# A fused graph and attention network on one core: the heads stage makes two steps of its side work per round in tiles 0 to 7

## The chip, the cores and the metric

The kernel runs on one NeuronCore of a Trainium2 chip. The core has a matrix engine (TensorE, in profiles PE, with its weight loads shown as PEld), VectorE (DVE), ScalarE (ACT), GpSimd (POOL) and SyncE (SP), which here only issues transfers. Each engine runs its own instructions in program order, and waits on semaphores for the others. The metric is the device time of one execution in microseconds; lower is better. A comparison is made on medians of several executions.

## The reference

The input is a node matrix `x` of 3327 x 256 and a symmetric 0/1 adjacency `adj` of 3327 x 3327. Four sublayers follow, each with a residual and a layernorm before it: a normalised graph convolution, a mixture of 8 experts with the top 2 chosen, a graph attention, and the last one, which concerns us, a causal attention with 4 heads of width 64, each with 4 query experts:

```python
sx = jnp.einsum('bsh,ndh->bnsd', x, hl_w) + hl_b[None, :, None, :]
q = jnp.einsum('bnsd,neod->bneso', sx, wq)      # 4 experts of queries per head
k = jnp.einsum('bnsd,nod->bnso', sx, wk)
v = jnp.einsum('bnsd,nod->bnso', sx, wv)
scores = jnp.einsum('bnesd,bntd->bnest', q, k) * d ** 0.5 + causal
qkv = jnp.einsum('bnest,bntd->bnesd', jax.nn.softmax(scores, axis=-1), v)
qkv = jnp.where(pad[:, :, None], 0.0, qkv)      # pad = (sx == 0)
gs = softmax(out @ gate_w + gate_b)             # gate over the 4 experts
mixed = jnp.einsum('bnsed,bnse->bnsd', out.reshape(b, nh, s, ne, d), gs)
hn = layernorm(mixed + resid, ln_g, ln_b)
# two dense layers on each head's 64 numbers with masks at exact zeros,
# a layernorm, and a softmax gate over the 4 heads
```

## The kernel before

The nodes are padded to 26 tiles of 128 rows (`NT` = 26, `P` = 128). The stages run one after another; the last, `heads` (line 773), takes the time from about 985 us to the end. All its instructions are recorded through `InOrder`, so every engine executes them in exactly the order in which the Python code issues them. For this reason almost all of them show the same line, L61, in the profile, and are told apart by tile names.

The work of the stage is a list of units, one for each tile `t` of 128 query rows and each of the 4 heads. A unit is cut into chunks of 512 keys (`BLK`), `t // 4 + 1` of them, because attention is causal: tiles 0 to 3 have one chunk per head and four per tile, tiles 4 to 7 have two per head and eight per tile, and so on, 392 in all. One turn of the main loop at line 1263, called a round here, handles chunk `k`, with several chunks in flight:

- `fill` (line 972): TensorE makes the scores of the 4 experts into four PSUM tiles `pqk`, from the tile's queries `qt` and the keys `kt`; the causal mask is added by small products (`own`, `after`).
- `drain` (994): VectorE copies each from PSUM to `sc` and takes the maximum on the way (the TENSOR_SCALAR_CACHE_REDUCE rows); at the unit's last chunk the maxima are joined to `anmax`.
- `weigh` (1014): ScalarE takes exp in place, with sums into `aden`.
- `values` (1028): SP issues the loads `vr<-vs` of the chunk's values from DRAM.
- `turn` (1035): VectorE transposes the weights in 32 x 32 blocks (STREAM_TRANSPOSE).
- `attend` (1047): TensorE multiplies them with the values into `po`.
- `over` (1066) at a unit's last chunk: ScalarE copies `po` to `ot`, and POOL multiplies by the mask `sxd`.
- `back` (1076), one round after it: TensorE turns `ot` back with the gate's weights (`ptO`), and ScalarE copies it to `qkv` and `glp`. At head 3 a tail is begun; before that, tails are run on until at most two are left.

The order in a round `k` is: the drains up to `wanted(k)` (three chunks ahead, more where a unit has more chunks), `attend` of chunk `k`, `turn` of chunk `k + 1`, `values` and half of `weigh` of chunk `k + 2`, `back` of a unit ended the round before, `over` of a unit ended now, a step of the side work, the rest of `weigh`, and a `fill` if none is waiting to be drained. `fill` of a tile's first chunk first calls `begin` (1217).

The side work is written as Python generators, and `run` (line 964) takes each of a list one step further, up to its next `yield`:

- `prepare(t)` (line 880), in the list `preps`, makes the projections of the next tile in 9 steps: 1 the load `xres` from DRAM; 2 layernorm statistics on VectorE and a root on POOL (`prs`); 3 the normalised rows `xn` on VectorE; 4 their transpose on TensorE (`pt`, copied to `xt`); 5 `psxt` and, on ScalarE, `sxt`; 6 four transfers to `sxd` and the product `pv` (copied to `v`); 7 `pk` (copied to `kt`) and four transfers of `v` to `vs` in DRAM; 8 `pq` (scaled into `qt`); 9 the compare that makes `sxd` a mask, and a transpose of `sxt` to `sx`. `begin` of a tile first runs `preps` to the end, and then begins the projections of the tile after it.
- `tail(t)` (line 1138), in `tails`, finishes a tile in 17 steps: the gate's softmax (`ard`, `glp`, `gl`, `gsm`, `gss`), the weighted sum over experts on POOL (`qkv`, `fx`), a layernorm (`l1st` on VectorE, the rest on POOL), two dense layers (`ph`, `h`, `fo`) with the masks, a second layernorm (`l2st`), the gate over heads (`fot`, `pfg`, `fgm`, `fgs`) with the residual's load `xend`, and the store of the result. Some steps are empty, to leave POOL time.

In tiles 0 to 7 the side work makes one step in every round; from tile 8 on, only in rounds that do not follow a unit's end. PSUM tiles of all these products (`pqk`, `pt`, `psxt`, `pv`, `pk`, `pq`, `ptO`, `ph`, `pfg`) share four buffers in rotation (pool `psm`), so each product waits until the fourth tile before it has been emptied. The helper `empty` (856) gives a copy out of PSUM to ScalarE or VectorE, by a running sum of costs that the code keeps.

Of the kernel before, what the change touches and what calls it, by code (L numbers as in the profile page):

```python
# [101 lines left out]
class Net:  # L102
# [670 lines left out]
    def heads(self, xs, vs, out):  # L773
# [3 lines left out]
        with ExitStack() as ctx:  # L777
# [186 lines left out]
            def run(gens):  # L964

                gens[:] = [g for g in gens if next(g, None) is None and g.gi_frame is not None]

            tails, preps, ready = [], [], {}
# [45 lines left out]
            def weigh(u, g, experts):  # L1014

                n = min(BLK, (u["t"] + 1) * P - g * BLK)
                q = ready[u["t"]]
                if u["h"] == g == 0 and 0 in experts:
                    q["den"] = sm.tile([P, 16, 7], F32, tag="den", name="aden", bufs=3)
                for k in experts:  # L1020
                    e = u["sc"][g][:, k, :n]
                    nc.scalar.activation(
                        e, e, AF.Exp, bias=u["nmax"][:, k : k + 1],
                        accum_out=q["den"][:, 4 * u["h"] + k, g : g + 1],
                    )
                    load["act"] += 0.26 + 0.00088 * n

            def values(u, g):

                n = 4 * min(4, u["t"] + 1 - 4 * g)  # L1030
                v = u["v", g] = vrp.tile([P, 16, 64], F32, tag="vr", name="vr")
                for q in range(4):
                    nc.sync.dma_start(out=v[ds(Q * q, Q), :n, :], in_=vs[u["h"], g, :, :n, :])

            def turn(u, g):


                n = min(BLK, (u["t"] + 1) * P - g * BLK)
                w = u["sc"][g][:, :, :n]
                nc.vector.transpose(w, w)  # L1040
                load["dve"] += 0.1 + 0.00417 * n
# [5 lines left out]
            def attend(u, g):  # L1047


                t = u["t"]  # L1050
                w, v = u["sc"][g], u["v", g]
                n = 4 * min(4, t + 1 - 4 * g)
                for b2 in range(0, n, 2):
                    for k in range(2):
                        for q in range(4):
                            r, b = ds(Q * q, Q), b2 + k

                            after = 4 * t + q - 16 * g
                            if b > after and t:
                                continue  # L1060
                            nc.tensor.matmul(
                                po[ds(64 * k, 64), q, :, :], v[r, b, :], w[r, :, ts(b, Q)],
                                start=(g == b2 == 0), stop=(b + 2 > after if t else b2 == 2),
                            )

            def over(u):

                u["ot"] = tl.tile([P, 4, P], F32, tag="ot", name="ot", bufs=1)
                nc.scalar.copy(u["ot"].rearrange("p e (q i) -> p q e i", q=4), po)
                nc.gpsimd.tensor_tensor(  # L1070
                    u["ot"], u["ot"],
                    u["sxd"][:, u["h"] : u["h"] + 1, :].to_broadcast([P, 4, P]), ALU.mult,
                )
                load["act"] += 0.6

            def back(u):


                h = u["h"]
                r = ready[u["t"]]  # L1080
                if h == 0:
                    r["qkv"] = tl.tile([P, 4, 4, 64], F32, tag="qkv", name="qkv", bufs=2)
                    r["glp"] = sm.tile([P, 4, 4, 4], F32, tag="glp", name="glp")
                pt = ps.tile([P, 4, 68], F32, tag="b", name="ptO")
                for e in range(4):
                    nc.tensor.matmul(
                        pt[:, e, :], u["ot"][:, e, :], igw[:, h, e, :], start=True, stop=True
                    )
                nc.scalar.copy(r["qkv"][:, h, :, :], pt[:, :, :64])
                nc.scalar.copy(r["glp"][:, h, :, :], pt[:, :, 64:])  # L1090
                load["act"] += 0.55
                if h == 3:
                    while len(tails) > 2:
                        run(tails)
                    tails.append(tail(u["t"], u["sx"], r["qkv"], r["glp"], r["den"]))
# [136 lines left out]
            def fill_next():  # L1232
                nonlocal filled
                if filled < len(chunks):
                    u, g = chunks[filled]
                    if g == 0:
                        begin(u)
                    fill(u, g)
                    filled += 1

            def drain_to(n):
                nonlocal drained
                while drained < min(n, len(chunks)):
                    if filled == drained:
                        fill_next()
                    drain(*chunks[drained])
                    drained += 1

            def wanted(k):

                return k + 3 + chunks[min(k + 2, len(chunks) - 1)][0]["t"] // 4
# [11 lines left out]
            for k, (u, g) in enumerate(chunks):  # L1263
                ahead = chunks[k + 2] if k + 2 < len(chunks) else None
                drain_to(wanted(k))
                attend(u, g)
                if k + 1 < len(chunks):
                    turn(*chunks[k + 1])
                if ahead:
                    values(*ahead)  # L1270
                    if ahead[1]:
                        weigh(*ahead, range(2))
                if ended:
                    back(ended)
                last = u if g == u["t"] // 4 else None
                if last:
                    over(u)
                if not ended or u["t"] < 8:
                    run(tails)
                    run(preps)  # L1280
                ended = last
                if ahead:
                    weigh(*ahead, range(2 if ahead[1] else 0, 4))
                if filled == drained:
                    fill_next()
# [556 lines left out]
```

## Time and profile before

| what | us |
|---|---|
| runs, not profiled | 3131.43, 3135.38, 3141.88 (median 3135.38) |
| the profiled execution's own time | 3144.19 |
| its span, first to last instruction | 3142.5 |
| PE busy | 2762.7 (88%) |
| DVE busy | 2494.8 (79%) |
| ACT busy | 1671.4 (53%) |
| POOL busy | 891.0 (28%) |

The span is what the profile's rows share out; 1.7 us of the execution's own time lie outside it. Busy time of an engine is the time with an instruction of its own in work. Matmuls are pipelined and their ends are modelled, so a high busy share of PE does not mean that PE sets the pace. PEclk is the share of full speed that TensorE's clock was granted.

### The profile page before, as it was taken

Reading aid. Unit: us, or ns where it says so; the run is one execution under the profiler, and the core shown is the slowest. Engines: PE = TensorE matmul, PEld = TensorE weight load, DVE = VectorE, ACT = ScalarE, POOL = GpSimd, SP = SyncE. Lnnn points to the kernel's source line nnn. Section 1 sums busy time; section 2 is a strip of 40 time slices with the busy share of each in tenths; the row PEclk is TensorE's granted clock in tenths of the full one; section 3 lists DMA queues with packets and bytes.
Section 4 is the critical chain, followed back from the end, with each engine's and each line's share of the span. In section 5 each row is a group of like instructions: output and inputs, shape, how many; then the busy total and the mean of one; then the engine's idle time right before and its main releaser. Section 6 shows DMA issues by size and latency. Waiting matters only on the chain.

```text
span 3142.5 us, 126717 instructions
## 1 busy us (share of the span) xinstructions
PE 2762.7 (88%) x54254; PEld 2025.9 (64%) x54254; DVE 2494.8 (79%) x6166; ACT 1671.4 (53%) x4566; POOL 891.0 (28%) x1208
## 2 busy tenths in 40 slices
PE   7999978688986879989999998889898899999884
PEld 6878877576775656666666666556665566656553
DVE  6104533799995768999998998899998899999994
ACT  6410145555553545666665665556655656566653
POOL 6432544611122353433322221121211111211112
PEclk9999999899998879999999999999999999999997
DMA  9994477476853313333333333333333333333331
GB/s 374 356 292 145 161 261 245 163 264 229 284 187 84 82 50 101 96 95 109 109 96 106 106 107 99 93 107 109 109 101 105 102 102 107 112 105 106 107 106 54
DMA packets 258193, 449.80 MB, mean 143 GB/s; under 512 B 58816, under 2 KB 159680, under 8 KB 257504
## 3 DMA queue, kind: packets, MB, share of 16 engines
q1 hardware_dynamic: 241232, 416.77, 43.5%
q0 software_dynamic: 6576, 18.02, 1.5%
q8 instruction: 428, 7.01, 1.0%
q10 hardware_dynamic: 9824, 6.91, 0.8%
q14 instruction: 133, 1.09, 0.1%
HBM read 393.37 MB, written 25.88 MB: 133 GB/s over the span
## 4 chain that ended last, share of the span: by engine, by line
DVE 37%; PE 23%; ACT 3%; issue 2%; POOL 1%; DMA 0%; SPq 0%; POOLq 0%; DVEq 0%; ACTq 0%
DVE sc L61 33%; PE po L61 10%; PE pqk L61 8%; PE ptO L61 2%; ACT sc L61 2%; PE pq L61 1%; DVE l2mv L61 0%; PE pt L61 0%; DVE gl L61 0%; PE psxt L61 0%; PE ph L61 0%; DVE l1mv L61 0%; DVE fo L61 0%; DVE l2st L61 0%; POOL fo L61 0%
## 5 line engine op out<-in xcount | busy, mean ns | idle before, releaser
L61 ACT ACTIVATE sc<-sc,anmax 128x512 f32<-128x512 f32 (+3 forms) x1568 | 1041.3, 671 | 125.1 <-DVE anmax L61 125.0
L61 DVE TENSOR_SCALAR_CACHE_REDUCE sc<-pqk 128x512 f32<-128x512 f32 (+3 forms) x1568 | 898.6, 627 | 110.6 <-PE pqk L61 109.2
L61 PEld LDWEIGHTS po<-sc,vr 32*64 32x64 f32 x43728 | 683.1, 134 | 369.8 <-DVE sc L61 203.5
L61 PE MATMUL po<-sc,vr 32*64 32x128 f32 x43728 | 789.0, 281 | 122.0 <-DVE sc L61 60.4
L61 PE MATMUL pqk<-kt,qt 64*128 64x512 f32 (+3 forms) x3136 | 832.5, 585 | 57.0 <-DVE fo L61 19.3
L61 DVE STREAM_TRANSPOSE sc<-sc 128x2048 f32<-128x2048 f32 (+3 forms) x392 | 816.0, 2082 | 11.5 <-ACT sc L61 11.3
L61 PEld LDWEIGHTS pqk<-kt,qt 64*128 64x128 f32 x3136 | 320.8, 188 | 295.8 <-issue 118.9
L61 PE MATMUL acc<-wh,p 128*128 128x259 f32 x1352 | 309.3, 386 | 34.4 <-DVE p L61 34.3
L61 POOL TENSOR_TENSOR ot<-ot,sxd 128x512 f32<-128x512 f32 x104 | 132.9, 1278 | 690.4 <-ACT ot L61 660.2
L61 PE MATMUL acc<-y,pan 128*128 128x256 f32 x1352 | 302.5, 384 | 12.3 <-DMA pan<-in_adjt_dram 10.6
L61 PEld LDWEIGHTS acc<-wh,p 128*128 128x128 f32 x1352 | 253.3, 190 | 92.6 <-DVE p L61 52.5
L61 ACT ACTIVATION_READ_ACCUMULATOR sc<-sc,anmax 128x1 f32 x1568 | 303.1, 193 | 0.0
L61 PEld LDWEIGHTS acc<-y,pan 128*128 128x128 f32 x1352 | 256.9, 192 | 53.4 <-issue 18.4
L61 ACT ACTIVATE u<-u,d 128x512 f32<-128x512 f32 (+1 forms) x182 | 125.2, 688 | 158.5 <-DVE u L61 158.3
L61 ACT COPY qkv<-ptO 128x256 f32<-128x256 f32 x104 | 38.7, 373 | 281.5 <-PE ptO L61 281.5
L61 DVE SCALAR_TENSOR_TENSOR u<-bc,d 128x512 f32<-128x512 f32 (+1 forms) x182 | 135.9, 747 | 0.1
L61 DVE SCALAR_TENSOR_TENSOR p<-pan,u 128x512 f32<-128x512 f32 (+1 forms) x182 | 125.8, 691 | 10.5 <-PE acc L61 6.1
L61 DVE DVE_READ_ACCUMULATOR sc<-pqk 128x1 f32 x1568 | 129.6, 83 | 0.0
L61 PE MATMUL ptO<-igw,ot 128*128 128x68 f32 x832 | 118.4, 286 | 11.5 <-DVE sc L61 4.4
L61 PEld LDWEIGHTS ptO<-igw,ot 128*128 128x128 f32 x832 | 103.8, 196 | 31.4 <-issue 21.8
L61 ACT ACTIVATE junk<-ar 128x1664 bf16<-128x1664 f32 x52 | 82.7, 1591 | 66.1 <-DMA ar<-in_adj_dram 64.8
L61 POOL TENSOR_TENSOR qkv<-qkv,gss 128x1024 f32<-128x1024 f32 x26 | 50.1, 1926 | 211.7 <-DVE gss L61 200.9
(286 smaller groups left out, 2870.2 us busy)
## 6 DMA issues: line engine op xcount, KB each, us to landing
vr<-vs SPq DMA_DIRECT2D x1248, 128.0 KB
ar<-in_adj_dram SPq DMA_DIRECT2D x104, 832.0 KB
pan<-in_adjt_dram SPq DMA_DIRECT2D x156, 256.0 KB
pan<-in_adjt_dram SPq DMA_DIRECT2D x26, 1024.0 KB
pan<-in_adjt_dram SPq DMA_DIRECT2D x20, 832.0 KB
w1e<-w SPq DMA_DIRECT2D x59, 256.0 KB
vr<-vs SPq DMA_DIRECT2D x96, 96.0 KB
took<-places SPq DMA_DIRECT2D x59, 129.0 KB
```

The source lines that it names most:

```text
L61: made = make(*args, **kw)
```

## The change

Behind `attend` and ahead of `turn`, in rounds of tiles 0 to 7, tails and projections make a step more. The step that was there, later in the round, stays.

```diff
                 drain_to(wanted(k))
                 attend(u, g)
+                if u["t"] < 8:
+                    run(tails)
+                    run(preps)
                 if k + 1 < len(chunks):
                     turn(*chunks[k + 1])
                 if ahead:
```

`run`, `tails` and `preps` are those described above. Nothing else of the kernel is edited. As `empty` decides by sums of costs so far, a few copies out of PSUM go to the other engine with the new order.

## The prediction

> **What bounds the kernel now.** I read the page first (VectorE, "DVE", is busy 79% of the span and carries 37% of the chain that ended last), then the busy time of each engine stretch by stretch, then VectorE's instructions in order of time. In the table by stretch I cut the heads stage at the first transpose (STREAM_TRANSPOSE) of each of the tiles 0 to 7; columns are length, then busy time per engine, granted clock, DMA share, GB/s.
>
> ```profile
> 1010.54:1033.42 22.88, 16.69 (x232) 13.13 (x229) 10.36 (x42) 10.52 (x42) 4.33 (x4) 0.78 0.29 67
> 1033.42:1058.66 25.24, 21.67 (x346) 17.13 (x346) 17.43 (x58) 14.62 (x52) 6.67 (x6) 0.86 0.29 75
> 1058.66:1089.48 30.82, 26.63 (x480) 19.64 (x480) 22.73 (x65) 17.25 (x55) 15.30 (x16) 0.89 0.30 82
> 1089.48:1125.05 35.57, 30.86 (x600) 23.13 (x602) 26.35 (x76) 19.04 (x57) 14.10 (x15) 0.86 0.24 64
> 1125.05:1193.59 68.54, 52.96 (x829) 38.75 (x820) 41.70 (x159) 27.95 (x99) 36.24 (x45) 0.75 0.22 59
> 1193.59:1235.21 41.62, 38.29 (x904) 27.51 (x898) 38.05 (x119) 27.19 (x90) 20.06 (x22) 1.00 0.36 101
> 1235.21:1282.74 47.53, 42.77 (x1031) 29.67 (x1030) 42.80 (x119) 28.95 (x91) 19.77 (x22) 1.00 0.37 100
> 1282.74:1332.97 50.23, 46.96 (x1154) 32.48 (x1154) 47.60 (x127) 30.85 (x91) 19.99 (x22) 1.00 0.36 103
> ```
>
> Tiles 5 to 7 are bound by VectorE (41.62 − 38.05 = 3.6, then 4.7 and 2.6 us idle). Tiles 0 to 4 are not: VectorE idles 12.5, 7.8, 8.1, 9.2 and 26.8 us, 64.4 in all, and TensorE's clock is 0.75 to 0.89 instead of 1.00. The whole change acts on these 322.4 us, a tenth of the kernel. Where the idle time lies is seen in VectorE's instructions in order of time (start, duration, what; in brackets idle time before it and who ended it):
>
> ```profile
> 1048.73 0.42 DVE L61 COPY kt<-pk 128x256 f32<-128x256 f32 x1 [4.90 <-PE pk L61]
> 1050.44 0.69 DVE L61 TENSOR_SCALAR qt<-pq 128x512 f32<-128x512 f32 x1 [1.28 <-PE pq L61]
> 1052.30 0.56 DVE L61 TENSOR_SCALAR_CACHE_REDUCE sc<-pqk 128x384 f32<-128x384 f32 x1 [0.84 <-PE pqk L61]
> ...
> 1079.39 0.43 DVE L61 TENSOR_SCALAR sxd<-sxd 128x512 f32<-128x512 f32 x1 [6.39 <-DMA sxd<-sxt]
> ...
> 1113.66 0.43 DVE L61 TENSOR_SCALAR sxd<-sxd 128x512 f32<-128x512 f32 x1 [6.59 <-DMA sxd<-sxt]
> ...
> 1146.01 0.42 DVE L61 TENSOR_TENSOR fo<-ph,fb 128x256 f32<-128x256 f32 x1 [4.51 <-PE ph L61]
> ...
> 1164.23 0.69 DVE L61 TENSOR_SCALAR_CACHE_REDUCE sc<-pqk 128x512 f32<-128x512 f32 x1 [5.75 <-PE pqk L61]
> ```
>
> The reader is to see one hole per tile at the place where `begin` finishes the next tile's projections in one go (the chain xt, psxt, sxt, pv, pk, pq, qt, one engine waiting for the next), and from 1133 to 1164 us a second kind: `back` runs three tails to make room for a fourth.
>
> **The change, part by part.** It adds and removes no work; it moves steps, and two products change engine. In each of the rounds of tiles 0 to 7 (4·4 + 4·8 = 48) tails and projections get a second step, issued behind `attend` and ahead of `turn`.
>
> *Projections, tiles 1 to 3 and into 4.* A projection has 9 steps. Four rounds lie between two calls of `begin` in tiles 0 to 3, so now 4 steps are spread and 5 are run at once; with two a round 8 are spread, and one (the compare on sxd, the transpose of sxt) is left. What goes at most is VectorE's idle time there: tile 1: 4.90 + 1.28 + 0.84 = 7.0; tile 2: 6.39 + 0.94 = 7.3; tile 3: 6.59 + 0.63 + 0.22 = 7.4; tile 4, where 8 rounds lay between: 4.19 + 1.54 + 0.39 = 6.1 us. Only two rounds precede the first `begin`: there 7 steps were left (waits 0.54 + 1.72 + 5.00 + 0.72 + 0.99 + 0.43 = 9.4), now 5, so 0.54 + 1.72 = 2.3 go. Sum 30.1.
>
> *Tails.* A tail has 17 steps. With one a round in rounds of 4 to a tile, three are unfinished when the fourth comes, and they are run out together. With two a round each is done in 9 rounds and `back` finds at most two. What goes at most: 1.47 + 2.52 + 0.22 + 4.51 = 8.7 of waits inside, and 5.75 + 0.58 = 6.3 at the end, where VectorE waits for pqk behind it. Sum 15.0. Both together 45.1 of the 75.4 us that VectorE idles in tiles 0 to 7.
>
> *What is late next.* (a) The last round of each projection on TensorE: attend 1.19, pk 1.23, ptO 1.1, pq 1.92, ACT's two qt of 0.60, and the first pqk 0.92 before VectorE has something to drain, 7.6 us; beside it VectorE has 4 drains of 0.47 and 0.16 for the maximum, the transpose 1.25 to 1.78, 0.65 of softmax and 0.42 for sxd, 4.6. 3.0 us stay idle for each of the four boundaries: 12. At the warm clock of tiles 5 to 7 they would be under 2 each; where TensorE stays as cold as in the holes (0.56 at 1043.8 to 1048.7) the round before it adds 1 to 2 (psxt 1.79, sxt 0.63, pv 1.22). Bounds 6 to 20. (b) xn now stands ahead of the transpose and half a round behind its statistics, and POOL makes its root behind the tail's normalisation (roots 1.02 and 0.56, products 0.62, 0.62, 0.73, 0.73: 4.3 us) while VectorE has 0.75 of statistics and 1.9 to 2.8 of drains. It waits about 1 us in tiles 2, 3 and 4, and transpose and `attend` behind it wait too. I take 3; bounds 0 and 14 (twice the one xn wait of the trace, 1.72, in each of tiles 2 to 5). (c) In tiles 5 to 7 there is nothing to fill but 10.9 us of idle time in 24 rounds, 0.45 a round; I take no gain and no loss. Bounds: 5 back (the waits for pqk there sum to 4.6) and 6 lost (half as much again as now).
>
> *SP and POOL.* SP issues a projection's 9 transfers (xres 0.42, four sxd of 0.605, four vs of about 0.5) and a tail's xend and out; half of them now precede the round's vr loads, which are for the chunk two rounds on, 7 us or more away: nothing. Without that cover it would be 2.4 us a tile. The xres that landed 2.1 us after its issue (1013.78, used 1015.92) is now read in its own round; SP reaches it ahead of the third chunk's vr loads, 2 us sooner, so nothing again. POOL's tail products now also stand ahead of `ot`; ptO, one round later, covers that. *Emptying PSUM:* VectorE loses one qt (0.69) and one kt (0.42) to ScalarE and gains one sx (about 0.4): −0.7, noise.
>
> *A rule against it.* In tiles 0 to 7 the seven `glp<-glp,ard` took 2.9 us in all where 225 ns is the median, and one of them 1.25, beside `ot` on POOL; with gss and the two roots' sums the excess is about 3.6 us, already in the rows. The Trainium skill, SBUF — State Buffer, "two separate sides", says that a VectorE operation with two SBUF inputs and a GpSimd operation lock a shared port pair, the loser blocked for the whole instruction. By that rule, if each of the 5 VectorE step groups of 7 tails met half an `ot` (0.64), the sum would lose 22 us. The trace shows a sixth of that with every step behind `ot`, and the change puts half of them ahead of it, so I add nothing.
>
> **Sum.** 45.1 − 12 − 3 = 30 us. The profiled execution took 3144.19 us (span 3142.5, 1.7 around it), so 3114; it lies 8.8 above the median of the runs, 3135.38, and on that scale the forecast is 3105. A difference under 0.3% (9.4 us) is about what a measurement of this kernel cannot tell from none; the three runs lie 10.5 apart.
>
> **The rivals.** *TensorE becomes the bound* (0.24). Its busy time in tiles 0 to 4 is 148.8 of 183.0 us; if the steps only move into a stream that is full, and it stays 92% busy as in tile 5, 148.8/0.92 = 161.7, gain 21, and 14 with (b) at its middle, 7: 3121. For it: 86% busy in tiles 1 to 3. Against: that busy time is counted at a clock of 0.75 to 0.89, and the holes are when the clock is low. The Trainium skill, TensorE: Matmul & The Clock Gate, "What's actually happening", gives half rate after an idle window of about 3.4 us and full rate after a busy one; by it tile 4 without its holes would run at the full clock, its 53.0 us of matmul would be 53.0·0.75 = 39.7, and this rival would fall away there. *The holes are hidden anyway or come back* (0.07): the tail work that leaves 1133 to 1164 and the projection's chain reappear as waits of the same length in each round. Then 3130 to 3140. Against: the 41 us lie on VectorE in seven places, nothing else of that length runs beside them. *Slower* (0.07): the new steps stand ahead of `turn` on VectorE and ahead of ptO and the fill on TensorE, both in program order. If a step there waits for ScalarE or POOL by about 1 us in each of the 48 rounds, 48 us are lost against 33 gained (45 − 12): 3150. It decides at 0.7 us a round. For it: rows such as `fo<-ph` 1.47 and `xn` 1.72 in the old place. Against: in tiles 5 to 7, where steps run every round, all VectorE waits together are 10.9 us in 24 rounds, under 0.5. *More than 45 back* (0.02): the warm clock shortens (a) to nothing.
>
> **How the numbers follow.** The likeliest, 0.60: gain 22 to 45, 3090 to 3113, centre 3105. To leave out two in ten, the range takes in the TensorE rival: from 3088 to 3126 (gain 9 to 47). Faster by over 0.3%: 0.60 + 0.24 + 0.02 = 0.86; within: 0.07; slower: 0.07.
>
> **What would show it.** Right: the length of tile 4 falls from 68.5 to about 41 us and tiles 1 to 3 lose 3 to 5 each; no wait of VectorE for sxd's DMA over 1 us; no stretch between 1100 and 1180 where TensorE's clock is 0.5; tiles 8 to 25 keep their lengths within 1%. (a) shows as waits of VectorE for pqk at tile boundaries of about 3 us, (b) as xn waiting for POOL's prs. Wrong: sc on VectorE waiting for pqk in most rounds of tiles 5 to 7, ACT or PE waiting for a step's result ahead of ptO, or a tile 0 to 4 that keeps its length with VectorE idle in smaller pieces.

## The result: no gain, and half a per cent lost

| | us |
|---|---|
| after, median of 5 runs | 3151.59 (3149.53 to 3159.35) |
| before, median of 5 runs beside them | 3135.38 (3131.43 to 3141.88) |
| ratio, with its 95% interval | 1.0053 (1.0033 to 1.0072) |
| profiled execution of after, and its span | 3159.35, 3157.6 (before 3144.19, 3142.5) |
| forecast | 3105 (3088 to 3126) |

The changed kernel is slower. The forecast was wrong in its sign, and its range misses the median by 26 us. The profiled executions lie 15.2 us apart, the medians 16.2.

**The profile after.** The table by stretch, cut as in the prediction (first transpose of each of the tiles 0 to 7; length, busy time of PE, PEld, DVE, ACT, POOL, granted clock, DMA share, GB/s):

```profile
1008.20:1027.89 19.69, 15.83 (x231) 12.61 (x231) 11.03 (x45) 9.69 (x39) 4.85 (x5) 0.83 0.33 81
1027.89:1053.35 25.46, 20.81 (x349) 16.02 (x348) 19.51 (x67) 16.30 (x57) 15.18 (x15) 0.97 0.35 89
1053.35:1087.21 33.86, 28.93 (x488) 20.67 (x488) 26.58 (x78) 18.29 (x57) 18.37 (x20) 0.85 0.29 79
1087.21:1124.23 37.02, 32.57 (x616) 22.63 (x616) 30.96 (x90) 20.44 (x62) 19.68 (x22) 0.91 0.27 70
1124.23:1179.86 55.63, 44.84 (x792) 33.88 (x793) 37.93 (x135) 25.95 (x89) 24.17 (x29) 0.79 0.24 61
1179.86:1230.04 50.18, 40.03 (x903) 29.12 (x902) 38.95 (x119) 27.26 (x90) 19.65 (x22) 0.93 0.31 84
1230.04:1283.32 53.28, 44.11 (x996) 30.48 (x1002) 44.31 (x119) 29.39 (x90) 19.68 (x22) 0.91 0.32 89
1283.32:1343.17 59.85, 51.55 (x1216) 36.10 (x1203) 47.70 (x127) 31.03 (x90) 19.65 (x22) 0.88 0.30 86
```

Line by line beside before: tile 0 is 3.2 us shorter, tiles 1 to 3 are 4.7 longer together, tile 4 is 12.9 shorter, and tiles 5 to 7, where before had nothing to gain, are 23.9 longer (163.31 for 139.39) while VectorE's work there grew by 2.5. Tiles 0 to 7 went from 322.4 to 335.0 us. The rest, tiles 8 to 25, which the change hardly touches, took 1770.0 for 1764.3; a second profile of before gave 1770.2, so that difference says nothing.

VectorE's busy and idle time share this out without a remainder. In tiles 0 to 4 its idle time fell from 64.5 to 45.7 us (−18.8, and 9.1 of it in tile 4). In tiles 5 to 7 it rose from 10.9 to 32.4 (+21.4). Its busy time in tiles 0 to 7 rose from 247.0 to 257.0 (+10.0). The sum is +12.6, against 30 less in the forecast.

The waits of over 2 us that are left in tiles 1 to 4 are others than before. VectorE's instructions in order of time in after (start, duration, what; in brackets the idle time ahead of it and who ended it):

```profile
1085.95 1.34 DVE L61 TENSOR_SCALAR xn<-xres,pmv,prs 128x256 f32<-128x256 f32 x1 [3.04 <-POOL prs L61]
...
1122.97 1.34 DVE L61 TENSOR_SCALAR xn<-xres,pmv,prs 128x256 f32<-128x256 f32 x1 [2.44 <-POOL prs L61]
...
1134.45 0.42 DVE L61 SCALAR_TENSOR_TENSOR h<-fxt,h 128x256 f32<-128x256 f32 x1 [3.46 <-ACT h L61]
...
1157.98 0.29 DVE L61 TENSOR_SCALAR_CACHE_REDUCE sc<-pqk 128x128 f32<-128x128 f32 x1 [2.87 <-PE pqk L61]
```

The waits for `sxd`'s transfer (6.4 and 6.6 us) and for `pk` (4.9) are gone, as the change was to bring. In their place stand waits for what the step before has only just given to POOL (`prs`) or to ScalarE (`h`). What keeps `prs` is seen in POOL's instructions in order of time, tile 2 of after, ahead of the first `xn` above (start, duration, what):

```profile
1076.39 1.03 POOL L61 TENSOR_TENSOR l2rs<-l2rs,nhalf 128x4 f32<-128x4 f32 x1 [0.45 <-DVE l2rs L61]
...
1080.27 1.27 POOL L61 TENSOR_TENSOR ot<-ot,sxd 128x512 f32<-128x512 f32 x1
1081.50 1.02 POOL L61 TENSOR_TENSOR l1rs<-l1rs,nhalf 128x4 f32<-128x4 f32 x1
...
1085.35 0.56 POOL L61 TENSOR_TENSOR prs<-prs,nhalf 128x1 f32<-128x1 f32 x1
```

POOL works without a gap from 1076.4 to 1085.9: the second normalisation of one tail, an `ot`, the first normalisation of another tail, and only then the projection's root. Two tails now make a step at the same time as the projection.

In tiles 5 to 7, these are the longest waits of TensorE and of VectorE in after (who waits for whom: us in all, times, longest):

```profile
PE pt L61 <- POOL fx L61: 14.4, 3, 5.2
PE pt L61 <- DVE xn L61: 3.7, 2, 2.1
...
DVE sc L61 <- PE pqk L61: 16.4, 18, 2.3
DVE l1st L61 <- POOL fx L61: 4.7, 3, 2.2
DVE h L61 <- ACT h L61: 3.0, 2, 2.2
```

The first, second, fourth and fifth are steps of the side work that wait for the step before them; before has none of these four over 0.3 us there. The third stands behind them: TensorE fills late, and VectorE's drains wait 16.4 us in 18 places (before 4.6 in 9). One case in order of time, tile 5 of after, and then the same two steps in tile 5 of before:

```profile
1200.81 0.23 DVE L61 BATCH_NORM_STATS2 l1st<-fx 128x6 f32<-128x64 f32 x1 [2.24 <-POOL fx L61]
...
1202.52 1.01 POOL L61 TENSOR_TENSOR l1rs<-l1rs,nhalf 128x4 f32<-128x4 f32 x1 [1.74 <-DVE l1rs L61]
...
1205.70 0.72 POOL L61 TENSOR_TENSOR fx<-fx,lnb 128x256 f32<-128x256 f32 x1
...
1206.48 0.69 PE L61 MATMUL pt<-ident,fx 128*128 128x128 f32 x2 [4.47 <-POOL fx L61]
...
1208.57 0.42 DVE L61 TENSOR_SCALAR_CACHE_REDUCE sc<-pqk 128x256 f32<-128x256 f32 x1 [1.47 <-PE pqk L61]
```

```profile
1220.72 0.18 DVE L61 BATCH_NORM_STATS2 l1st<-fx 128x6 f32<-128x64 f32 x1
...
1231.26 0.42 PE L61 MATMUL pt<-ident,fx 128*128 128x128 f32 x2
```

POOL's normalisation of `fx` takes from 1202.5 to 1206.4 us, a root and four products. The tail leaves it a distance of two steps, one of them empty. With one step in a round of tiles 5 to 7 (139.39 us for 24 rounds in before, 5.8 each) these are two rounds; with two, one. The transpose `pt` is then at the head of TensorE's queue, 4.47 us early, and the scores behind it wait too. In time the distance shrinks by more than half. From the start of the tail's statistics on VectorE (`l1st`) to the moment when TensorE stands at `pt` it is 10.5, 13.7 and 13.8 us in the three tiles of before, and 1.2, 0.5 and 0.9 in after, where 5.7 are needed: VectorE comes late to the statistics, having waited for POOL's sum `fx`, and on TensorE only the `attend` of the next round stands in between, whose transpose VectorE had made ahead of the statistics.

### The profile page after: what moved, and what is told of

Its sections match the earlier page's. It is cut to its first block, busy times and chain, and to the rows that moved or that the text cites. A ratio compares the mean times of both kernels' runs of the same rounds, so it can differ in the third digit from the quotient of the medians.

```text
span 3157.6 us, 126764 instructions
## 1 busy us (share of the span) xinstructions
PE 2765.5 (88%) x54254; PEld 2025.2 (64%) x54254; DVE 2501.9 (79%) x6165; ACT 1673.3 (53%) x4567; POOL 886.0 (28%) x1208
## 4 chain that ended last, share of the span: by engine, by line
DVE 34%; PE 24%; ACT 3%; issue 3%; POOL 2%; DMA 0%; SPq 0%; POOLq 0%; DVEq 0%; ACTq 0%
DVE sc L61 29%; PE po L61 10%; PE pqk L61 9%; ACT sc L61 2%; PE ptO L61 2%; POOL fx L61 1%; PE pt L61 1%; POOL qkv L61 1%; PE pq L61 1%; PE ph L61 0%; DVE l2mv L61 0%; PE psxt L61 0%; POOL fo L61 0%; DVE fo L61 0%; DVE gl L61 0%
## 5 line engine op out<-in xcount | busy, mean ns | idle before, releaser
L61 PE MATMUL pqk<-kt,qt 64*128 64x512 f32 (+3 forms) x3136 | 841.8, 593 | 48.8 <-DVE fo L61 14.7
L61 DVE SCALAR_TENSOR_TENSOR p<-pan,u 128x512 f32<-128x512 f32 (+1 forms) x182 | 126.2, 694 | 10.6 <-PE acc L61 6.2
L61 PE MATMUL ptO<-igw,ot 128*128 128x68 f32 x832 | 118.9, 286 | 12.6 <-issue 5.0
L61 PEld LDWEIGHTS ptO<-igw,ot 128*128 128x128 f32 x832 | 104.9, 197 | 30.8 <-issue 21.4
## 6 DMA issues: line engine op xcount, KB each, us to landing
vr<-vs SPq DMA_DIRECT2D x1248, 128.0 KB
```

Source lines behind the costliest of these rows:

```text
L61: made = make(*args, **kw)
```

## The experiments

Two theories came out of this reading, and the expectations speak of them. **Spacing** (S): two steps in a round come before POOL and ScalarE have made what the second needs, wherever in the round they stand. **Place** (P): a step ahead of `turn`, of ptO or of `over` holds up what is queued behind it, even if it comes alone. Lengths of the tiles by the profile of each run, in us:

| kernel | tile 0 | 1 to 3 | 4 | 5 to 7 | 0 to 7 | ratio to before (95%) |
|---|---|---|---|---|---|---|
| before | 22.9 | 91.6 | 68.5 | 139.4 | 322.4 | |
| before, second profile | 22.6 | 92.3 | 65.5 | 140.6 | 321.0 | |
| after | 19.7 | 96.3 | 55.6 | 163.3 | 335.0 | 1.0053 (1.0033–1.0072) |
| preps_only | 22.1 | 91.5 | 61.5 | 146.9 | 322.0 | 1.0022 (1.0005–1.0038) |
| tails_only | 22.7 | 99.8 | 61.6 | 164.1 | 348.2 | 1.0105 (1.0083–1.0128) |
| slack | 21.9 | 80.4 | 49.6 | 150.8 | 302.8 | 0.9951 (0.9936–0.9967) |
| one_early | 21.5 | 90.8 | 76.2 | 155.7 | 344.1 | 1.0070 (1.0052–1.0088) |
| one_behind | 22.6 | 97.2 | 76.4 | 160.7 | 356.9 | 1.0140 (1.0117–1.0163) |
| behind_turn | 21.7 | 99.8 | 60.0 | 164.6 | 346.0 | 1.0086 (1.0066–1.0106) |
| slack_behind | 21.9 | 81.7 | 50.8 | 165.0 | 319.4 | 1.0018 (1.0001–1.0034) |
| one_ahead_ot | 23.0 | 107.0 | 72.1 | 163.9 | 365.9 | 1.0144 (1.0125–1.0163) |
| tails_ahead_ot | 22.6 | 109.3 | 72.7 | 159.7 | 364.3 | 1.0137 (1.0109–1.0165) |
| preps_ahead_ot | 23.2 | 93.9 | 65.1 | 146.3 | 328.5 | 1.0018 (1.0003–1.0033) |
| two_late | 25.3 | 98.1 | 60.0 | 172.6 | 355.9 | 1.0101 (1.0082–1.0119) |
| slack_late | 25.6 | 99.0 | 57.1 | 153.2 | 334.9 | 1.0028 (1.0012–1.0044) |
| slack_late_to4 | 25.5 | 97.5 | 55.3 | 140.2 | 318.5 | 0.9985 (0.9970–1.0000) |
| slack_to4 | 22.1 | 80.4 | 52.6 | 140.0 | 295.1 | 0.9943 (0.9924–0.9962) |
| slack_to3 | 22.4 | 79.3 | 50.8 | 151.6 | 304.0 | 0.9955 (0.9942–0.9969) |

The two profiles of before give the scatter of this table: 3 us in tile 4, about 1 in the other columns. Tiles 8 to 25 lie between 1757 and 1780 us in these profiles, so the tile columns carry the reading, and the ratios confirm it.

### The two lists apart

Only the projections make the new step (**preps_only**), or only the tails (**tails_only**):

```diff
                 if u["t"] < 8:
-                    run(tails)
                     run(preps)
```

> Only the projections make the second step behind attend; tails keep one step a round. Theory S (spacing: two steps a round come before POOL or ScalarE have made what the next step needs): projections ask POOL for one root only, so the holes where begin finished them (7.0, 7.3, 7.4 and 6.1 us of VectorE in tiles 1 to 4) go and tiles 5 to 7 stay at 41.6, 47.5 and 50.2 us within 2; about 3115 to 3122. Theory P (place: any step ahead of the transpose and of ptO in program order holds up the round): tiles 5 to 7 grow by 2 to 4 us each, 3132 to 3145.

```diff
                 if u["t"] < 8:
                     run(tails)
-                    run(preps)
```

> Only the tails make the second step behind attend; projections keep one step a round. Theory S: the tails carry the loss: tiles 5 to 7 grow by about the 24 us that they grew in the changed kernel, of which tile 4 without its run-out of three tails gives back 12 to 15, and the holes of the projections stay; 3145 to 3160, slower than the changed kernel. Theory P: loss shared between tails and projections, so between before and changed: 3138 to 3148.

Measured: 3149.05 and 3173.45 us beside 3142.44 of before. The tails carry the loss: in tiles 5 to 7 tails_only is 24.7 us longer than before, as long as after. The projections alone cost 7.5 there, and they bring nothing in tiles 1 to 3 (91.5 for 91.6), though the hole at the tile's boundary is closed. Theory S has the sharing between the lists right, but its times were too low (3115 to 3122 and 3145 to 3160), and so were those of P. preps_only in order of time shows where the gain goes; VectorE's waits at the boundary, then POOL, VectorE and TensorE some rounds on:

```profile
1043.47 0.42 DVE L61 COPY sx<-pt 128x256 f32<-128x256 f32 x1 [0.96 <-PE pt L61]
...
1044.80 0.56 DVE L61 TENSOR_SCALAR_CACHE_REDUCE sc<-pqk 128x384 f32<-128x384 f32 x1 [0.91 <-PE pqk L61]
...
1050.03 1.91 POOL L61 TENSOR_TENSOR qkv<-qkv,gss 128x1024 f32<-128x1024 f32 x1
...
1052.01 1.27 POOL L61 TENSOR_TENSOR qkv<-qkv 128x512 f32<-128x512 f32 x1
...
1054.84 0.55 POOL L61 TENSOR_TENSOR prs<-prs,nhalf 128x1 f32<-128x1 f32 x1
...
1055.42 1.34 DVE L61 TENSOR_SCALAR xn<-xres,pmv,prs 128x256 f32<-128x256 f32 x1 [3.75 <-POOL prs L61]
...
1056.91 0.66 PE L61 MATMUL pt<-ident,xn 128*128 128x128 f32 x2 [5.24 <-DVE xn L61]
```

At the boundary 7.0 us of waits have become 1.9. But the projection's root `prs` stands on POOL behind the tail's weighted sum (1.91 and 1.27 us, and two more products), `xn` waits 3.75 us for it, takes 1.34 us itself, beside an `ot` of POOL, where it takes 0.41 with POOL idle, and TensorE waits 5.24 us. What was saved at one place is paid at another in the same tile.

### Spacing

The new step stays, and each of a tail's four pauses is lengthened from a distance of two steps to one of four (**slack**). Nothing else is edited, so a pause is again about as long in rounds as in before. The edit at each of the two-step pauses:

```diff
-                yield
-                yield
+                for _ in range(4 if t < 7 else 2):
+                    yield
```

> The changed kernel, with the four pauses of a tail (two empty steps behind each group of POOL products) made four steps long for tails of tiles 0 to 6, so that in rounds they are as long as before. Theory S: TensorE no longer waits for fx (14.4 us in tiles 5 to 7 of the changed kernel, 3 waits) and tiles 5 to 7 fall from 163 us to 140 to 148; 3125 to 3137. Theory P: the steps stay ahead of the transpose, tiles 5 to 7 stay at 155 to 163 us; 3145 to 3152.

Measured: 3127.52 us, ratio 0.9951, so faster than before by 0.5%; after's median, taken at another time, is 24 us longer. All parts are shorter than in after: tiles 1 to 3 from 96.3 to 80.4, tile 4 from 55.6 to 49.6, tiles 5 to 7 from 163.3 to 150.8. TensorE's longest waits in tiles 5 to 7 of slack:

```profile
PE po L61 <- ACT sc L61: 4.3, 2, 2.6
PE pqk L61 <- DVE sc L61: 3.3, 1, 3.3
...
PE ptO L61 <- POOL ot L61: 1.4, 2, 0.7
```

The 14.4 us of `pt` waiting for POOL's `fx` are gone (8.6, 7.7 and 8.5 us now lie between the statistics and `pt`); nothing in the place of the step was changed. So spacing is shown as a cause, worth 15.9 us in tiles 1 to 3, 6.0 in tile 4 and 12.5 in tiles 5 to 7. In tiles 5 to 7, 10.6 of the 12.5 are idle time of VectorE and 1.9 its work, some of which the longer tails put off (tiles 8 and 9 have 1.0 more). But 11.4 us of the 23.9 lost there remain, more than S allowed (140 to 148 us).

### Place

One step in a round as in before, but moved. **one_early** has it at the change's place, behind `attend`. **one_behind** has it behind `turn`, so VectorE's transpose is no longer behind it. **behind_turn** and **slack_behind** are after and slack with the new step behind `turn`. **one_ahead_ot** has the one step last of all ahead of `over`, behind `back`.

one_early is after without the later step:

```diff
-                if not ended or u["t"] < 8:
+                if not ended and u["t"] >= 8:
                     run(tails)
                     run(preps)
```

> One step a round as before, but at the new place, behind attend and ahead of the transpose; the later place is left out for tiles 0 to 7. Theory S: a full round lies between steps, as before, so 3130 to 3140 and tiles 5 to 7 at 139 us in all, within 4. Theory P: about half of the changed kernel's loss in tiles 5 to 7 (12 us) shows here without the gain in tile 4: 3143 to 3150.

```diff
                 attend(u, g)
-                if u["t"] < 8:
-                    run(tails)
-                    run(preps)
                 if k + 1 < len(chunks):
                     turn(*chunks[k + 1])
+                if u["t"] < 8:
+                    run(tails)
+                    run(preps)
```

This edit alone makes behind_turn of after and slack_behind of slack; together with the one before it makes one_behind.

> One step a round, behind the transpose instead of ahead of it (and ahead of values and ptO); the later place is left out for tiles 0 to 7. It differs from the run with one step behind attend by the transpose alone. Theory P, narrowed: VectorE's part of a step (up to 2.1 us) ahead of the transpose holds up attend, then the fill, then the drain; here tiles 5 to 7 return from 155.7 us to 139 to 144 and the time to 3133 to 3143. If it is TensorE's part ahead of ptO and the fill that costs, they stay at 150 to 156 and the time near 3160.

> The changed kernel with its new step behind the transpose instead of ahead of it; two steps a round. Spacing alone: the waits of TensorE for fx stay (14 us in tiles 5 to 7), tiles 5 to 7 150 to 160 us instead of 163; 3138 to 3150. Place alone: tiles 5 to 7 fall to 140 to 147, 3120 to 3132.

> Both undone: the tails' pauses of four steps, and the new step behind the transpose. If spacing and place are two causes that add up, tiles 5 to 7 fall from 150.8 us (pauses alone) to 138 to 144 and tiles 0 to 4 stay near 152; about 3110 to 3120. If place costs nothing once the pauses are there, it stays at 3125 to 3130.

```diff
                 if ended:
                     back(ended)
+                if u["t"] < 8:
+                    run(tails)
+                    run(preps)
                 last = u if g == u["t"] // 4 else None
                 if last:
                     over(u)
-                if not ended or u["t"] < 8:
+                if not ended and u["t"] >= 8:
                     run(tails)
                     run(preps)
```

(The change's step behind `attend` is not in it.)

> One step a round, behind ptO and the first half of weigh, but ahead of over, so ahead of ScalarE's copy of po and POOL's product ot; otherwise as before, where it stands behind over. If place costs through TensorE's products ahead of ptO and the fill, or through ScalarE's copies ahead of weigh, tiles 5 to 7 are back at 139 to 144 us and the time at 3133 to 3143. If it costs through POOL's and ScalarE's work of the step ahead of ot, they stay at 150 us or more and the time at 3150 or more.

Measured: with one step a round and the pauses of before, each of the three places costs tiles 5 to 7 16.3, 21.3 and 24.5 us. So place is a cause as well, without any doubling, and a dearer one than expected (one_early 3163.94 for 3143 to 3150). That `empty` gives copies to another engine is not what the runs differ by: in tiles 5 to 7 of before, after, slack and all these runs with one step, ScalarE makes every one of the 26 or 27 copies. My narrower form of it, that a step holds up VectorE's transpose, fell: moved behind `turn` the same step cost more, not less (one_behind 1.0140 against one_early 1.0070, behind_turn 1.0086 against after's 1.0053, slack_behind 1.0018 against slack's 0.9951). slack_behind was to show two causes that add up, with 138 to 144 us in tiles 5 to 7; it takes 165.0.

What the three places share is `over`, which stands behind them all. To see which list it is, the step ahead of `over` was split: only the tails' there (**tails_ahead_ot**), or only the projections' (**preps_ahead_ot**), the other behind `over` as in before.

The edit of tails_ahead_ot against before (in preps_ahead_ot `tails` and `preps` change places):

```diff
                 if ended:
                     back(ended)
+                if u["t"] < 8:
+                    run(tails)
                 last = u if g == u["t"] // 4 else None
                 if last:
                     over(u)
-                if not ended or u["t"] < 8:
+                if not ended and u["t"] >= 8:
                     run(tails)
+                if not ended or u["t"] < 8:
                     run(preps)
```

> One step a round; the tails' step ahead of over, the projections' behind it as before. If POOL's products of a tail, queued ahead of ot, make the cost of place, this run has nearly all of the 24 us that tiles 5 to 7 lost with both ahead (139.4 to 163.9): 156 to 164, TensorE waiting for ot 8 us or more there; 3160 to 3185. If it is ScalarE's copies, most of which are the projections', tiles 5 to 7 take 140 to 148.

> One step a round; the projections' step ahead of over, the tails' behind it as before. Mirror of the run before it: POOL: tiles 5 to 7 at 139 to 145 us, 3133 to 3148; ScalarE's copies: 152 to 164 us, 3155 to 3180.

Measured: tails_ahead_ot loses 20.4 us in tiles 5 to 7, preps_ahead_ot 6.9, where both together lost 24.5. So most of the cost at this place is the tails', as the expectation by POOL's queue has it, though both times and the 146.3 us of preps_ahead_ot lie a little over its ranges. POOL's queue in tails_ahead_ot, and at the end TensorE, in order of time:

```profile
1238.26 1.02 POOL L61 TENSOR_TENSOR l2rs<-l2rs,nhalf 128x4 f32<-128x4 f32 x1 [3.04 <-DVE l2rs L61]
1239.25 0.62 POOL L61 TENSOR_TENSOR fo<-fo,l2mv 128x256 f32<-128x256 f32 x1
...
1241.44 0.72 POOL L61 TENSOR_TENSOR fo<-fo,fnb 128x256 f32<-128x256 f32 x1
1242.12 1.26 POOL L61 TENSOR_TENSOR ot<-ot,sxd 128x512 f32<-128x512 f32 x1
...
1243.44 1.98 PE L61 MATMUL ptO<-igw,ot 128*128 128x68 f32 x8 [4.51 <-POOL ot L61]
```

A tail's normalisation (3.9 us with its root) now stands on POOL ahead of the `ot` of the unit that has just ended. `ot` is not late because POOL is full, but because it is behind work that nobody needs soon; ptO, the next thing that TensorE has in its order, waits 4.51 us for it. In tiles 5 to 7 ptO waits for POOL's `ot`:

| kernel | us |
|---|---|
| before, after, behind_turn, preps_ahead_ot | none |
| tails_ahead_ot | 12.0 |
| one_ahead_ot | 12.5 |
| one_behind | 9.8 |
| slack_behind | 13.7 |
| one_early | 2.4 |
| slack | 1.4 |

In one_behind, slack_behind, one_ahead_ot and tails_ahead_ot this is about half of the loss. behind_turn loses 25.2 us without it; there `pt` waits 14.1 us for `fx`, as in after. At the change's own place it is a small part: one_early loses 16.3 us with 2.4 of this wait. The longest waits of ScalarE and one of TensorE in tiles 5 to 7 of one_early:

```profile
ACT fot L61 <- PE pt L61: 15.5, 3, 7.7
...
ACT v L61 <- PE pv L61: 13.3, 3, 5.6
...
PE po L61 <- ACT ot L61: 5.5, 6, 1.4
```

In before, ScalarE waits there for `ptO` (46.9 us in 12 places) and for no product of a step by more than 1.9 us in all. Here it stands with a step's copy at the head of its queue, 15.5 and 13.3 us, while the step's product is behind `attend` on TensorE, and the exps of the round stand behind that copy. Whether this makes the 16.3 us was not tried by a run of its own; how they are shared out stays open.

### Both steps in the old place

If place costs, both steps could stand behind `over`: **two_late**, before with the step made twice; **slack_late**, the same with the longer pauses; **slack_late_to4**, with the second step and the longer pauses in tiles 0 to 4 only (`< 5` in place of `< 8` below, and pauses of tails 0 to 3).

```diff
                 if not ended or u["t"] < 8:
                     run(tails)
                     run(preps)
+                if u["t"] < 8:
+                    run(tails)
+                    run(preps)
```

> Two steps a round, both at the old place behind over. Place is as before, spacing as in the changed kernel or closer: TensorE waits for fx in tiles 5 to 7 (12 us or more), these take 148 to 158 us, tiles 0 to 4 about 170; 3135 to 3150.

> Two steps a round, both at the old place behind over, and the pauses of four steps for tails of tiles 0 to 6. Both causes undone: tiles 5 to 7 at 139 to 145 us, tiles 0 to 4 at 150 to 158; 3108 to 3120. If tiles 5 to 7 stay at 150 as with the pauses alone, place is not what keeps them there.

> As the run before it, but the second step only in rounds of tiles 0 to 4, and the long pauses for tails of tiles 0 to 3: a candidate for the fastest. Tiles 0 to 4 at 150 to 158 us, tiles 5 to 7 at 139 to 142; 3108 to 3120, the same as with the second step behind attend in these tiles (3121.5) within 6.

Measured: two_late is the slowest of all in tiles 5 to 7 (172.6): steps that follow each other directly wait for each other. The longer pauses take 19.3 us of this back (153.2), but in tiles 1 to 3 both stay at 98 to 99 us, over before's 91.6. slack_late, with both causes thought undone, was expected at 139 to 145 us in tiles 5 to 7 and 150 to 158 in tiles 0 to 4 (181.7 measured). slack_late_to4 is back at 140.2 in tiles 5 to 7, but its tiles 0 to 4 take 178.3 and its ratio of 0.9985 is hardly a gain. In slack_late what waits is the step that follows directly: TensorE's transpose for the `xn` of the step just ahead (first line, tiles 1 to 3), statistics for the rows that the step ahead of them has asked for, and `ph` for a copy of the same round (the others, tiles 5 to 7):

```profile
PE pt L61 <- DVE xn L61: 10.4, 3, 4.1
...
DVE pst L61 <- DMA xres<-xs: 7.6, 3, 3.0
...
PE ph L61 <- ACT fxt L61: 4.1, 3, 1.7
```

So a second place in the round, half a round away, is worth having for its distance: in tiles 1 to 3 slack (two places) takes 80.4 us, slack_late (one place) 99.0, with the same pauses.

### Only where there is something to fill

In tiles 5 to 7 VectorE was idle for 10.9 us and a step a round was enough. **slack_to4** is slack with the new step in tiles 0 to 4 only, and the longer pauses in tails 0 to 3; **slack_to3** has the same pauses and the step in tiles 0 to 3 (`< 4`). slack_to4 against slack:

```diff
-                for _ in range(4 if t < 7 else 2):
+                for _ in range(4 if t < 4 else 2):
                     yield
...
-                if u["t"] < 8:
+                if u["t"] < 5:
                     run(tails)
                     run(preps)
```

> The pauses of four steps for tails of tiles 0 to 3, the new step ahead of the transpose, and only in rounds of tiles 0 to 4, where VectorE has holes. Both theories: tiles 0 to 4 near 152 us as with the pauses alone, tiles 5 to 7 back at 139 to 143; 3108 to 3120. If the gain of tiles 0 to 4 is only put off, tiles 5 to 7 stay above 148.

> The long pauses for tails of tiles 0 to 3 and the second step behind attend only in rounds of tiles 0 to 3. If the second step costs in tile 4 what it costs in tiles 5 to 7, tile 4 falls from 52.6 us to 40 to 46 and the time to 3108 to 3117, the fastest; if tile 4 needs it to work off the tails, it stays at 52 or more.

Measured: slack_to4 has the lowest ratio of the study, 0.9943 (3121.52 us beside 3138.74), but its interval overlaps those of slack (0.9951) and slack_to3 (0.9955), so that it is faster than these is not shown by the times. Tiles 0 to 7 take 295.1 us in its profile, 27.3 less than before; the medians differ by 17.2, and tiles 8 to 25, at 1772.3, give some of it back or only scatter. Its stretches for tiles 1 to 5, with the columns of the table by stretch:

```profile
1031.79:1051.91 20.12, 19.81 (x346) 15.60 (x346) 17.09 (x58) 15.01 (x53) 10.32 (x9) 1.00 0.37 93
1051.91:1078.15 26.24, 25.50 (x485) 18.77 (x484) 23.87 (x69) 18.08 (x59) 14.23 (x15) 1.00 0.37 101
1078.15:1112.20 34.05, 31.25 (x616) 23.40 (x616) 28.51 (x85) 20.26 (x64) 18.55 (x21) 0.90 0.28 71
1112.20:1164.78 52.58, 48.03 (x803) 36.70 (x802) 42.63 (x147) 26.47 (x93) 28.95 (x35) 0.84 0.26 71
1164.78:1208.29 43.51, 36.03 (x887) 26.48 (x886) 36.53 (x112) 26.50 (x89) 19.61 (x22) 1.00 0.36 96
```

Tiles 1 and 2 run at the full clock with TensorE busy 98% and 97% of the time, against 85% and 91% for VectorE; there TensorE is now the nearer bound, as the prediction's first rival has it. Tile 5 is back at about its old length (43.5 for 41.6) and its old clock. slack_to3 is not better: tile 4 takes 50.8 us, between the two expectations, and tiles 5 to 7, whose rounds are as in slack_to4, take 151.6 us. No one wait makes these: VectorE waits 14.3 us in 12 places for pqk (5.0 at most), where slack_to4 has 5.4 in 10. That the long tails, run at one step a round in tile 4, reach further into them is likely, but was not tried.

### A second profile of before

**before_again** is the kernel before, profiled once more for the scatter of the table above.

> The kernel before, unchanged, for a second profile: all theories expect tiles 0 to 7 within 4 us of 322.4; how far tiles 8 to 25 lie from 1764.3 us (10 either way, say) is the scatter of a single profile, against which the 6 to 16 us that other runs show there are to be read.

Tiles 0 to 7 took 321.0 us (322.4), tiles 8 to 25 1770.2 (1764.3).

## Why the prediction was wrong, point by point

The forecast for tiles 0 to 7 was 30 us less and they took 12.6 more. 18.6 of the difference lie in tiles 0 to 4, which became 11.4 us shorter instead of 30, and 23.9 in tiles 5 to 7, which were to stay as they were.

*What goes at most: right as a reading, wrong as a sum.* The holes do go: no VectorE wait for `sxd`'s transfer is left, and where a tile's projections end and its first pqk is drained VectorE waits 0.91 and 0.67 us (tiles 2 and 3) and under 0.2 (tiles 4 and 5), so step (a), 12 us, was set far too high. What kept the gain small is (b) and the work of the tails, below. Tile 4 fell by 12.9 us, with 9.1 of idle time of the 21.1 that I counted there (15.0 and 6.1). The tail steps that now come in pairs wait in it for `h` (3.46, 2.50) and the drains for pqk (2.87, 2.67).

*Step (b), xn waiting for POOL's root: the mechanism right, the size off.* I took 3 us and bounded it by 14. Measured 7.6 us in 4 waits, and the `xn` themselves grew by 2.2 us. In the rounds of the three longest TensorE stands waiting for `fx` (1.5 to 1.8 us) and for `xn` (1.3 to 1.6), and VectorE's next drain waits 0.95, 2.34 and 1.16 us more. That makes 12 us, four times what I took, though within the bound. `prs` stands on POOL behind two tails' normalisations and an `ot`, 9.0 us in a row, where I had written one normalisation of 4.3 us; in preps_only, behind the weighted sum. The drains that wait behind it were not in the sum.

*Step (c), "no gain and no loss" in tiles 5 to 7, bounds 5 back and 6 lost: this is the step that failed.* VectorE's idle time there rose by 21.4 us, 3.5 times the bound. I had bounded a new wait by the waits of the trace, but in that trace a tail's pause was worth two rounds. The change halves that distance in rounds. Setting POOL's 3.9 us for `fx`, and 1.7 for the statistics ahead of them, against one round of 5.8 would not have shown the loss, for they just fit. The distance in time fell to 0.5 to 1.2 us in these tiles, as the rows above show. Before had one row that shows the price, in tile 4, where `back` runs the tails on step after step and a pause is worth no round:

```profile
1138.11 0.69 PE L61 MATMUL pt<-ident,fx 128*128 128x128 f32 x2 [2.41 <-POOL fx L61]
```

I had not set it against the tiles behind. The pauses are half of this step's failure: with them lengthened, 12.5 of the 23.9 us go. What makes the other 11.4 is place, and at the change's own place how it does so stays open.

*"POOL's tail products now also stand ahead of `ot`; ptO, one round later, covers that": right for this change, and no further.* ptO has no such wait in after, 1.4 us of it in slack and 2.4 in one_early. With one step behind `turn` or `back`, or two with the longer pauses behind `turn`, it waits 9.8 to 13.7 us.

*The tail's work was moved, not only its waits.* With tails twice as fast, VectorE's busy time in tiles 0 to 3 rose from 76.9 to 88.1 us, and fell in tile 4 by 3.8 and in tiles 8 and 9 by 3.8. I had charged tiles 0 to 3 with nothing.

*The rule against it, "I add nothing": wrong in sign, right in doubting 22 us.* The three groups of VectorE instructions in tiles 0 to 7 of after that grew most (count, busy us, mean ns of one, idle before):

```profile
L61 DVE TENSOR_SCALAR xn<-xres,pmv,prs 128x256 f32<-128x256 f32 x9 | 6.5, 719 | 7.6 <-POOL prs L61 7.6
L61 DVE TENSOR_TENSOR gl<-gl,gateb 128x16 f32<-128x16 f32 x7 | 4.7, 676 | 0.2
...
L61 DVE TENSOR_TENSOR gss<-gss,gsm 128x16 f32<-128x16 f32 x7 | 3.7, 527 | 0.2
```

In before their means were 490, 205 and 329 ns (3.9, 1.4 and 2.3 us, with one `xn` fewer, 0.4 us). That is about 7 us more, on the engine that sets the pace, against the 22 that the rule of the Trainium skill, SBUF — State Buffer, "two separate sides", gave if each step group met half an `ot`. The row has the rule's sign, and a third of its size.

*The rivals.* "Slower", at 0.07, is what came: a step that waits for POOL or ScalarE by about 1 us in each round. In tiles 5 to 7 it is 23.9 us in 24 rounds, 1.0 a round. That the rival's price, 3150, is so near the median, 3151.6, is luck: it set 48 us lost against 33 gained, and the profiles have 28.6 lost (tiles 1 to 3 and 5 to 7) against 16.1 gained. Its place was put rightly too ("ahead of ptO and the fill on TensorE"). What I set against it, under 0.5 us of waits a round in tiles 5 to 7 where steps run in every round, was evidence from steps at twice the distance and in another place. "TensorE becomes the bound" came near only in tiles 1 and 2 of the kernels with longer pauses in the change's own place (98% and 97% busy in slack_to4), where the waits are out of the way.

*The marks that I had set.* Tile 4 to about 41: it fell to 55.6. Tiles 1 to 3 to lose 3 to 5 each: they grew by 4.7 together. No stretch at half the clock between 1100 and 1180: there are three (from 1123.4, 1154.1 and 1171.1, each at 0.50). No wait for `sxd`'s transfer over 1 us, and tiles 8 to 25 within 1%: both came. "sc on VectorE waiting for pqk in most rounds of tiles 5 to 7", named as what would show it wrong: 18 waits in 14 of the 24 rounds, 0.9 us each in the mean.

## What to carry to other kernels

Where a side chain is spread over the rounds of a main loop, its pauses are a time for other engines, counted in rounds; whoever runs the chain twice as fast must look up what each pause covers, and set it against the time from the one engine's start to the moment when the next engine stands at the result, not against rounds alone (here 10.5 to 13.8 us became 0.5 to 1.2), and lengthen the pauses if it is not enough (slack_to4: the same edit with longer pauses, limited to the tiles that have idle time, is 0.57% faster than before where the edit alone is 0.53% slower). On an engine that is 28% busy, order still matters: a root and four products that nobody needs yet, ahead of the one that TensorE waits for, cost up to 4.5 us a time, 12.0 us in tiles 5 to 7 (tails_ahead_ot). A stretch with little idle time of the engine that bounds it has little to gain from more side work in each round, and is best left out of the edit.

## What the runs showed of the hardware

A VectorE operation of 16 numbers per partition, `gl<-gl,gateb`, took 676 ns in the mean of after and 205 in before. Three of the seven in after took 1.23 to 1.28 us, each beside an `ot` of POOL; with POOL idle it took 0.17 to 0.18. `xn`, which has only one tensor as its input, beside scalars for each partition, went from 0.41 to 1.34 us beside `ot`, so not only operations with two tensor inputs meet this; beside POOL's roots (`l2rs`) it stayed at 0.41.

The clock that TensorE was granted in tiles 5 to 7 is 1.00 in each stretch of before, and 0.93, 0.91 and 0.88 in after. Towards the end of each of the three waits for `fx` there (4.5 to 5.2 us) it falls to 0.50 for 6.8 us, from 1205.3, 1256.5 and 1311.1, and the same four products of pqk (64x384) that took 0.92 us ahead of the second wait took 1.65 behind it; in slack_to4, without these waits, the clock is 1.00 again. So waits of that length cost clock as well as their own time. A few hundredths can have other causes: the second profile of before has 0.97 in tile 7 with no wait of TensorE over 1.6 us. TensorE's busy time in tiles 5 to 7 rose from 128.0 to 135.7 us; how much of the 23.9 us is the clock's was not separated.
